# Layer 2 of the last sample as side steps of layer 3, with layer 3's preparation on one PSUM bank

## The chip, the core and the metric

The kernel runs on one core of one Trainium2 chip. The metric is the device time of one execution in microseconds (us). The kernel before took 10504.44 us, the median of three runs (10501.73, 10504.44 and 10507.75).

The engines are named as in the profile: PE is TensorE (matmul), DVE is VectorE, ACT is ScalarE, POOL is GpSimd, SP is SyncE, which here issues all DMAs. Each engine works through its own queue in order, and waits at an instruction until what it needs is there.

## What is computed

Four layers on images x of shape (4 samples, 128 channels, 64 x 64 pixels), in float32. Cut to what matters here:

```
# layer 2, for each sample, n = 4096 pixels
f, g, hh = Wf x + bf, Wg x + bg, Wh x + bh        # 1, 1 and 128 rows of n
attn = softmax(f[i] * g[j], over j)               # n x n, rank one before the softmax
out  = hh @ attn + x                              # bcj,bji->bci

# layer 3: two Mamba scans over all 4 x 4096 pixels as one sequence, forward and backward
u, z  = split(Win x);  u = silu(conv(u, 4 taps) + conv_b)
dt, B, C = Wx u;  delta = softplus(Wdt dt + bdt)
h[l] = exp(delta[l] A) * h[l-1] + delta[l] B[l] u[l]    # 256 channels x 16 states
y = (C . h + D u) * silu(z);  y = Wout y
out = silu(groupnorm(y_forward + y_backward)) + x       # groups of one sample
```

The forward scan of layer 3 reads the samples in order 0, 1, 2, 3. It needs the last sample's layer 2 only in its last quarter.

## The kernel before

**The scan stream** (scan_stream, L715) is used by layers 1 and 3. The work is cut into blocks of 128 rows by 1024 pixels (8 channels x 16 states). For block i, in this order: ACT copies the last column of h of block i-2 to `carry` (carried, L811); PE spreads the inputs of block i+1 to a PSUM pair of banks, `db` (spread, L749; two such pairs); ACT makes `da` of block i+2, an exponential (decayed, L758; three buffers), or, of each fourth block ("apart"), turns `db` itself into the decay (decayed_apart, L762); SP loads the row of block i+3 (load_for, L774; five buffers); DVE multiplies `db` with `b_rep` and runs the scan into `h` (four buffers); POOL multiplies row with `b_rep` to `x` for the apart blocks (driven, L783) and h with `c_rep` to `p` (seven buffers); PE sums p of four blocks into `total` with the matrix `gather` (summed, L795). After each block the caller's `side` runs, and before each scan its `early`. In these both, steps of other work are put into the engines' queues at places that are written out by hand or taken from a queue of steps. The order on each engine is the order of the program.

**Layer 1** has 256 blocks per sample. Beside them run the next window's preparation, the finished window's output (finish, L1149), and layer 2 of the sample before: pass_a (L1432), run eight times in finish, makes g, h, f and the extremes of g for 512 pixels each; row_weights (L1471), beside layer 0 of the next sample, makes the sums of the softmax; attend (L1511), beside layer 1 of the next sample, makes the 256 exponentials of 128 x 512 and their 256 matmuls, 16 results `res` on DVE, and stores to x3. The last sample has no next one, so finish leaves pass_a out for it, and layer2 (L1593) runs between layer 1 and layer 3 by itself: it loads the whole sample, makes g and h, and then, for 32 groups of 128 pixels, one exponential of 128 x 4096 on ACT with its sum, and eight f32 matmuls of 512 columns into eight PSUM banks, and at the end eight additions and eight stores to x3.

**Layer 3** (L1671) loads its weights (weights3, L1642: 47 small and middle-sized DMAs on SP, 32 of them for A_log), prepares chunk 0, and streams 32 chunks of 1024 pixels, 16 forward and 16 backward, each as two parts j of 16 blocks. A chunk is prepared (prep, L1717) beside the chunk before it; a table gives the block in which each step is issued. For each j: four taps of the convolution in two halves of 512 pixels and a Silu from PSUM (u); the rows of B, C and dt (bc); the time step with Softplus from PSUM (de, delta); the gate z with Silu from PSUM; then time_steps (L863), in steps: `du = delta u` on POOL, the stores of `d`, a copy of 32 rows, the first cast to bfloat16 (`high`), two rounds of remainders on PE and ACT (`minus`, `rest`), and `parted`, 12 DMAs of `split` to `parts`. Silu and Softplus need other ACT tables than the exponentials of the stream, so each of the six visits has two ACT_TABLE_LOADs, and uses two PSUM banks (ps1, two buffers). post (L1817) makes the output of the chunk before, and for the backward half finish reads y3 of a whole sample back, makes the group norm and stores the result; its buffers come from a pool `scratch` of two.

Of the kernel before, what the change touches and what calls it, by code (L numbers as in the profile page):

```python
# [16 lines left out]
P = 128  # L17
# [98 lines left out]
class Net:  # L116
# [186 lines left out]
    def weights12(self):  # L303
# [4 lines left out]
        self.load_rows(pool, ["bf", "bg", "bh"])  # L308
# [406 lines left out]
    def scan_stream(self, pools, blocks, side, early=lambda k, n: None):  # L715
# [95 lines left out]
        def carried(i):  # L811
            B, g = of(i)
            act.copy(B.carry[:, g : g + 1], h[i][:, B.at : B.at + 1])
            del h[i]
# [7 lines left out]
        for i, (k, n) in enumerate(items):  # L822
            B, g = of(i)
            if i > 1:
                carried(i - 2)
# [17 lines left out]
            pool.tensor_tensor(p[i], h[i], B.c_rep, ALU.mult)  # L843
            if n == 6 and k + 1 < len(blocks):
                blocks[k + 1].reps()
# [203 lines left out]
    def fetched(self, pool, b):  # L1049
        x = pool.tile([P, L], F32, name=f"x_{b}", tag="x")  # L1050
        for c in range(NCH):
            s = bass.ts(c, NB)
            self.nc.sync.dma_start(out=x[:, s], in_=self.x2[b % 2, :, s])
        return x


    def layer1(self, b):
# [12 lines left out]
        with self.pool("l1", 1) as big, self.pool("l1c", 2) as work, self.pool("l1t", 2) as tmp, \  # L1070
# [31 lines left out]
            def prepared(w):  # L1102
# [30 lines left out]
                for i in range(SG):  # L1133
# [3 lines left out]
                    g.way, g.at = slice(None), W - 1  # L1137
# [11 lines left out]
            def finish(w):  # L1149
# [26 lines left out]
                if not last:  # L1176
                    for c in range(C):
                        steps += self.pass_a(b, w * C + c, lambda c=c: held["x"][:, bass.ts(c, NB)], misc, tmp)
# [414 lines left out]
    def layer2(self, b, x):  # L1593
        nc = self.nc
        NT = L // P
        with self.pool("l2", 1) as big, self.pool("l2t", 2) as tmp, self.pool("l2e", 3) as ep:
            g = big.tile([P, L], F32, name="g", tag="g")
            hT = big.tile([P, NT, P], F32, name="hT", tag="hT")
            fcol = big.tile([P, NT], F32, name="fcol", tag="fcol")
            ntop = big.tile([P, NT], F32, name="ntop", tag="ntop")  # L1600
            gx = big.tile([P, 2, NCH], F32, name="gx", tag="gx")
            gm = big.tile([P, 2], F32, name="gm", tag="gm")
            with self.pool("l2p", 4, True) as ps4:
                for c in range(NCH):
                    s = bass.ts(c, NB)
                    ps = ps4.tile([P, NB], F32, name="g_ps", tag="misc")
                    nc.tensor.matmul(ps, self.wg_rep, x[:, s], start=True, stop=True)
                    nc.scalar.activation(g[:, s], ps, AF.Identity, bias=self.bg)
                    nc.vector.tensor_reduce(gx[:, 0, c : c + 1], g[:, s], AX.X, ALU.max)
                    nc.vector.tensor_reduce(gx[:, 1, c : c + 1], g[:, s], AX.X, ALU.min)  # L1610
                for t in range(NT):
                    ps = ps4.tile([P, NB], F32, name="h_ps", tag="misc")
                    nc.tensor.matmul(ps[:, 0 : P + 1], x[:, bass.ts(t, P)], self.WhfT, start=True, stop=True)
                    nc.vector.tensor_tensor(hT[:, t, :], ps[:, 0:P], self.bh, ALU.add)
                    nc.vector.tensor_tensor(fcol[:, t : t + 1], ps[:, P : P + 1], self.bf, ALU.add)
            nc.vector.tensor_reduce(gm[:, 0:1], gx[:, 0, :], AX.X, ALU.max)
            nc.vector.tensor_reduce(gm[:, 1:2], gx[:, 1, :], AX.X, ALU.min)

            nc.vector.tensor_scalar(ntop, fcol, gm[:, 0:1], None, ALU.mult)
            nc.vector.scalar_tensor_tensor(ntop, fcol, gm[:, 1:2], ntop, ALU.mult, ALU.max)  # L1620
            nc.vector.tensor_scalar(ntop, ntop, -1.0, None, ALU.mult)

            with self.pool("l2a", 1, True) as ps1:
                accs = [ps1.tile([P, NB], F32, name=f"acc{c}", tag=f"acc{c}") for c in range(NCH)]
                for t in range(NT):
                    e = ep.tile([P, L], F32, name="e", tag="e")
                    z = tmp.tile([P, 1], F32, name="z", tag="z")
                    nc.scalar.activation(
                        e, g, AF.Exp, bias=ntop[:, t : t + 1], scale=fcol[:, t : t + 1], accum_out=z,
                    )  # L1630
                    nc.vector.reciprocal(z, z)
                    nc.vector.tensor_scalar(hT[:, t, :], hT[:, t, :], z, None, ALU.mult)
                    for c in range(NCH):
                        nc.tensor.matmul(accs[c], hT[:, t, :], e[:, bass.ts(c, NB)], start=(t == 0), stop=(t == NT - 1))
                for c in range(NCH):
                    s = bass.ts(c, NB)
                    o = tmp.tile([P, NB], F32, name="o", tag="o")
                    nc.vector.tensor_tensor(o, accs[c], x[:, s], ALU.add)
                    nc.sync.dma_start(out=self.x3[:, b * L + c * NB : b * L + (c + 1) * NB], in_=o)


# [28 lines left out]

    def layer3(self):  # L1671
# [4 lines left out]
        with self.pool("l3w", 1) as big, self.pool("l3", 2) as work, self.pool("l3t", 2) as tmp, \  # L1676
                self.pool("l3x", 2) as scr, self.pool("l3u", 3) as st, self.pool("l3r", 2) as rows, \
                self.pool("l3p", 2, True) as ps1, self.pool("l3q", 2, True) as psd, \
                self.pool("l3s", 1, True) as pst:
# [14 lines left out]
            def scratch(name):  # L1694
                return scr.tile([P, T], F32, name=name, tag="s")
# [4 lines left out]
            def fetch(K):  # L1700

                lo = K.ch * T
                K.xt = work.tile([P, T + H], F32, name="xt", tag="xt")
                first, end = (lo - H, lo + T) if K.forward else (lo, lo + T + H)
                a, z = max(first, 0), min(end, N)
                if a > first:
                    dve.memset(K.xt[:, 0 : a - first], 0.0)
                if z < end:
                    dve.memset(K.xt[:, z - first : T + H], 0.0)
                sp.dma_start(out=K.xt[:, a - first : z - first], in_=self.x3[:, a:z])  # L1710

            def behind(K):

                K.yf = work.tile([P, T], F32, name="yf", tag="yf", bufs=1)
                sp.dma_start(out=K.yf, in_=self.y3[:, K.ch * T : (K.ch + 1) * T])

            def prep(K):  # L1717
# [3 lines left out]
                K.u = {}  # L1721

                def taps(j, c):
                    def go():
                        if c == 0:
                            K.u[j] = K.blocks[j].u = work.tile([P, T], F32, name="u", tag="u", bufs=3)
                        held["u", c] = misc("u_ps")
                        for i in range(self.K3):
                            o = c * NB + (i if K.forward else H - i)
                            pe.matmul(  # L1730
                                held["u", c], self.Wk[:, i, bass.ts(j, P)], K.xt[:, o : o + NB],
# [4 lines left out]
                def gate(j):  # L1736
                    def go():
                        if j == J - 1:
                            K.sz = work.tile([P, J, T], F32, name="sz", tag="sz")
                        for c in range(C):  # L1740
                            o = own + c * NB
                            held["z", c] = misc("z_ps")
# [345 lines left out]
```

## Time and profile before

| what | value |
|---|---|
| median of the three runs | 10504.44 us |
| profiled execution, span from its first to its last instruction | 10494.9 us |
| around the span, against the median of the runs | 9.5 us |
| mean granted TensorE clock | 0.903 |
| layer 1, first to last scan, samples 0, 1, 2, 3 | 861.3, 886.1, 883.6, 869.0 us |
| layer 3, first to last scan | 3463.9 us |
| DVE busy in layer 3 (6951 on): scans with `db`, products, scans apart | 1802.2, 926.8, 597.5 us |
| ACT_TABLE_LOADs of the whole kernel | 617 of 1283 ns |

How it is read: the profile's page gives, for one execution, the busy time of each engine, and the same in 40 slices of equal length (a digit 9 is 90% or more). Beside the page the trace can be asked for windows (busy time by engine in a stretch), for the timeline (start, duration, and in brackets the idle time before it and what ended it), for groups of equal instructions (count, busy time, mean duration, idle time before), and for waits. All times are in us from the first instruction. Nearly all rows carry the line L111, where a helper records every operation, so rows are told apart by their tiles. An f32 matmul leaves two records in the trace.

### The profile page before, as it was taken

Reading aid. Unit: us, or ns where it says so; the run is one execution under the profiler, and the core shown is the slowest. Engines: PE = TensorE matmul, PEld = TensorE weight load, DVE = VectorE, ACT = ScalarE, POOL = GpSimd, SP = SyncE. Lnnn points to the kernel's source line nnn. Section 1 sums busy time; section 2 is a strip of 40 time slices with the busy share of each in tenths; the row PEclk is TensorE's granted clock in tenths of the full one; section 3 lists DMA queues with packets and bytes.
Section 4 is the critical chain, followed back from the end, with each engine's and each line's share of the span. In section 5 each row is a group of like instructions: output and inputs, shape, how many; then the busy total and the mean of one; then the engine's idle time right before and its main releaser. Section 6 shows DMA issues by size and latency. Waiting matters only on the chain. (4 is left out here: it accounts for less than half of the span.)

```text
span 10494.9 us, 91078 instructions
## 1 busy us (share of the span) xinstructions
PE 8443.5 (80%) x28013; PEld 3021.6 (29%) x28088; DVE 9159.8 (87%) x6318; ACT 6387.1 (61%) x9576; POOL 8156.1 (78%) x3574
## 2 busy tenths in 40 slices
PE   8996667997887997887898887877777777777775
PEld 3331213332223333223333222322222222222221
DVE  7869998887998886999886999359999999999996
ACT  3334545666665665666665776456666666677765
POOL 6758896766887775888674888149999999989986
PEclk9997788998998999998999999888988989888886
DMA  1018882007885005887102888158888888888896
GB/s 37 12 37 201 194 194 85 18 14 189 211 203 149 15 14 129 201 213 191 33 16 63 206 211 200 32 133 199 207 198 206 204 202 208 215 223 224 228 227 176
DMA packets 512313, 1552.75 MB, mean 148 GB/s; under 512 B 84017, under 2 KB 91825, under 8 KB 511825
## 3 DMA queue, kind: packets, MB, share of 16 engines
q1 hardware_dynamic: 511824, 1546.92, 58.9%
q8 instruction: 223, 3.65, 0.2%
q14 instruction: 266, 2.17, 0.1%
HBM read 1349.40 MB, written 137.48 MB: 142 GB/s over the span
## 5 line engine op out<-in xcount | busy, mean ns | idle before, releaser
L111 POOL TENSOR_TENSOR p<-h,c_rep 128x1024 f32<-128x1024 f32 x2048 | 4807.9, 2359 | 734.8 <-DVE h L111 673.7
L111 DVE TENSOR_TENSOR_SCAN h<-da,carry,db 128x1024 f32<-128x1024 f32 x1536 | 3603.4, 2346 | 200.5 <-ACT da L111 17.8
L111 PE MATMUL db<-parts,sel 96*128 96x512 bf16 x4096 | 1401.5, 428 | 1460.3 <-DVE h L111 1408.2
L111 ACT ACTIVATE da<-row,A 128x1024 f32<-128x1024 f32 x1536 | 1761.1, 1147 | 359.4 <-DMA row<-d 341.0
L111 DVE TENSOR_TENSOR db<-b_rep,db 128x1024 f32<-128x1024 f32 x1536 | 1853.5, 1207 | 112.1 <-PE db L111 92.0
L111 POOL TENSOR_TENSOR e<-e,bound 128x1024 f32<-128x1024 f32 x512 | 1241.3, 2427 | 573.5 <-DVE e L111 573.0
L111 POOL TENSOR_TENSOR x<-row,b_rep 128x1024 f32<-128x1024 f32 x512 | 1208.8, 2361 | 123.8 <-DMA row<-d 122.8
L111 DVE TENSOR_TENSOR_SCAN h<-db,carry,x 128x1024 f32<-128x1024 f32 x512 | 1194.9, 2334 | 62.9 <-ACT db L111 35.3
L111 PE MATMUL total<-p,gather 128*32 128x512 f32 x8192 | 1225.7, 719 | 9.8 <-POOL p L111 9.8
L111 ACT ACTIVATE db<-db,A 128x1024 f32<-128x1024 f32 x512 | 555.3, 1085 | 1080.6 <-PE db L111 1026.5
L111 ACT ACTIVATE e<-e 128x1024 f32<-128x1024 f32 x512 | 540.9, 1057 | 1051.9 <-POOL e L111 1051.8
L111 PEld LDWEIGHTS <-sel 96*128 96x128 bf16 x4096 | 309.6, 101 | 3002.0 <-DVE h L111 2017.3
L111 PE MATMUL lg<-q,k 128*128 128x512 f32 x2048 | 1021.5, 623 | 106.5 <-DVE e L111 98.3
L111 PE MATMUL acc<-t,vT 128*128 128x512 f32 x2048 | 964.1, 595 | 3.3 <-DVE t L111 3.3
L111 PE MATMUL acc<-e,values 128*128 128x512 f32 x1536 | 854.9, 648 | 88.8 <-ACT e L111 62.9
L111 DVE TENSOR_TENSOR t<-lg,ncut 128x1024 f32<-128x1024 f32 x512 | 624.5, 1220 | 288.1 <-PE acc L111 264.0
L111 ACT ACT_TABLE_LOAD x617 | 791.6, 1283 | 38.8 <-DMA r<-y 12.3
L111 ACT ACTIVATE e<-gq,below,fcol 128x512 f32<-128x512 f32 x768 | 610.2, 805 | 87.0 <-PE acc L111 86.7
L111 POOL TENSOR_TENSOR t<-t,e 128x1024 f32<-128x1024 f32 x256 | 610.4, 2384 | 45.4 <-ACT t L111 45.4
L111 ACT ACTIVATE junk<-gp,ntop,fcol 128x512 f32<-128x512 f32 x768 | 619.5, 807 | 30.4 <-DMA gp<-g 17.7
L111 ACT COPY carry<-h 128x1 f32<-128x1 f32 x2048 | 373.5, 185 | 416.4 <-DVE h L111 411.4
L111 DVE SCALAR_TENSOR_TENSOR e<-t,lg 128x1024 f32<-128x1024 f32 x512 | 618.5, 1208 | 1.2
(259 smaller groups left out, 9927.5 us busy)
## 6 DMA issues: line engine op xcount, KB each, us to landing
row<-d SPq DMA_DIRECT2D x2048, 512.0 KB
parts<-split SPq DMA_DIRECT2D x912, 64.0 KB
b_rep<-bc SPq DMA_DIRECT2D x96, 512.0 KB
c_rep<-bc SPq DMA_DIRECT2D x96, 512.0 KB
d<-delta SPq DMA_DIRECT2D x76, 384.0 KB
r<-y SPq DMA_DIRECT2D x48, 512.0 KB
xq<-in_x SPq DMA_DIRECT2D x72, 256.0 KB
res<-x SPq DMA_DIRECT2D x32, 512.0 KB
```

Of the source, the lines that this page charges most:

```text
L111: return self.tc.keep_in_program_order(method(*args, **kwargs))
```

## The change

Five things are changed together.

1. layer2 and its loader are removed. finish of layer 1 runs pass_a for the last sample too. A new function, layer2_beside, does the rest as side steps of layer 3's forward blocks: 128 exponentials of 128 x 1024 with their sums (store), a logarithm, then 256 exponentials of 128 x 512 and 256 f32 matmuls, two rounds of eight results, with loads from g2, h2, x2 and x3 and stores to x3. A list `busy` estimates ACT's time in each of the 32 blocks of a chunk, and a step is issued when the estimate leaves room in 3.3 us per block (up to 4.0 saved up). By the built order the 128 are issued in chunks 0 to 5 (22, then 26 in each of 1 to 4, then 2) and the 256 in chunks 5 to 11.
2. Its accumulator takes a PSUM bank of its own (psa), so layer 3's preparation has one bank instead of two. Each half of 512 is copied out by ACT at the beginning of a later block (`first`, a new hook of scan_stream), before the next half is made.
3. Of the six table visits per chunk, each two for u, delta and z become one: the halves are copied with their bias, and the function is then applied to whole tiles. So there are three visits, with six ACT_TABLE_LOADs instead of twelve.
4. In the forward half, the copy to `carry` is made by POOL, after p of block i, instead of ACT before it (512 copies of 128 x 1).
5. Buffers: xt 2 to 1, split of layer 3 2 to 1, `scratch` as two tags of one buffer each, yf used as the exponentials' buffer in the forward half; the steps of prep, post and finish are moved in their tables (`du` at blocks 16 and 18 instead of 15 and 21, the store of the chunk before at 11 instead of 8), and finish reads a sample's four parts in the opposite order.

```diff
-        self.load_rows(pool, ["bf", "bg", "bh"])
+        self.load_rows(pool, ["bf", "bh"])
+        self.load_rows(self.const, ["bg"])
...
         def carried(i):
             B, g = of(i)
-            act.copy(B.carry[:, g : g + 1], h[i][:, B.at : B.at + 1])
+            keep = pool.tensor_copy if B.carry_on_pool else act.copy
+            keep(B.carry[:, g : g + 1], h[i][:, B.at : B.at + 1])
             del h[i]
...
+            first(k, n)
-            if i > 1:
+            if i > 1 and not of(i - 2)[0].carry_on_pool:
                 carried(i - 2)
...
             pool.tensor_tensor(p[i], h[i], B.c_rep, ALU.mult)
+            if i > 1 and of(i - 2)[0].carry_on_pool:
+                carried(i - 2)
...
-                if not last:
-                    for c in range(C):
-                        steps += self.pass_a(...)
+                for c in range(C):
+                    steps += self.pass_a(...)
...
+    def layer2_beside(self, b, keep, e, g, psa, busy, per):
...
+        def steps():
+            load_row(0)
...
+            dve.tensor_scalar(ntop, fcol, gm[:, 0:1], None, ALU.mult)
+            dve.scalar_tensor_tensor(ntop, fcol, gm[:, 1:2], ntop, ALU.mult, ALU.max)
+            dve.tensor_scalar(ntop, ntop, -1.0, None, ALU.mult)
+            yield later(3)
+            for c in range(NW):
+                for t in range(NT):
+                    yield 1.42
+                    if t == HALF and c + 1 < NW:
+                        load_row(c + 1)
+                    act.activation(
+                        store[:, 1, :], row(c), AF.Exp, bias=ntop[:, t : t + 1], scale=fcol[:, t : t + 1],
+                        accum_out=sums[:, t, c : c + 1],
+                    )
...
+                for v in range(h * NCH, (h + 1) * NCH):
+                    for t in range(HALF):
+                        yield 0.81
+                        if t == HALF // 2:
+                            load_res(v)
+                            if v + 1 < 2 * NCH:
+                                load_part(v + 1)
+                        at = h * HALF + t
+                        act.activation(
+                            half(e, t), half(g, v), AF.Exp, bias=below[:, at : at + 1], scale=fcol[:, at : at + 1],
+                        )
+                        now["due"].append((v, t))
+
+        def product(v, t):
+            if t == 0:
+                acc[v] = psa.tile([P, NB], F32, name="acc", tag="acc")
+            pe.matmul(acc[v], values[:, t, :], half(e, t), start=(t == 0), stop=(t == HALF - 1))
...
+        def early(i):
+            v = now["full"]
+            if v is not None:
+                dve.tensor_tensor(res, acc.pop(v), res, ALU.add)
...
+            due, now["due"] = now["due"], []
+            for u in due:
+                product(*u)
+            now["left"] = min(now["left"] + per - busy[i % len(busy)], 4.0)
+            while now["need"] is not None and i >= now["from"] and now["need"] <= now["left"] and len(now["due"]) < 2:
+                now["left"] -= max(now["need"], 0)
+                now["need"] = next(run, None)
...
-                self.pool("l3x", 2) as scr, self.pool("l3u", 3) as st, self.pool("l3r", 2) as rows, \
-                self.pool("l3p", 2, True) as ps1, self.pool("l3q", 2, True) as psd, \
-                self.pool("l3s", 1, True) as pst:
+                self.pool("l3x", 1) as scr, self.pool("l3u", 3) as st, self.pool("l3r", 2) as rows, \
+                self.pool("l3v", 1) as keep, self.pool("l3p", 1, True) as ps1, self.pool("l3a", 1, True) as psa, \
+                self.pool("l3q", 2, True) as psd, self.pool("l3s", 1, True) as pst:
...
+                def whole(func, dst, last, bias):
+                    s = bass.ts(C - 1, NB)
+                    for j in (0, 1):
+                        if j != last:
+                            act.activation(dst(j), dst(j), func)
+                    rest = dst(last)[:, 0 : (C - 1) * NB]
+                    act.activation(rest, rest, func)
...
+                        act.activation(dst(last)[:, s], held["ps"], func, bias=bias[:, last : last + 1])
+                    self.exp_tables(act)
...
-                    0: [taps(0, 0)], 2: [taps(0, 1)], 3: [silu(0, "u")],
-                    7: [taps(1, 0)], 10: [taps(1, 1)], 11: [silu(1, "u")],
-                    12: [rows_a], 13: [rows_b], 14: [step_a(0), step_b(0)], 15: [rows_c, todo(0, 0)],
-                    16: [step_a(1), step_b(1)], 17: [todo(0, 1)],
-                    18: [gate(1), silu(1, "z")], 21: [todo(0, 2), todo(0, 3), todo(1, 0)],
-                    22: [todo(0, 4)], 23: [todo(0, 5), todo(1, 1)], 24: [todo(0, 6)],
-                    25: [todo(0, 7), todo(1, 2), todo(1, 3)], 26: [todo(0, 8), gate(0), silu(0, "z")],
-                    28: [todo(1, 4)], 29: [todo(1, 5)], 30: [todo(1, 6)], 31: [todo(1, 7)],
-                }, {1: [todo(1, 8)]}
+                first = {
+                    2: [u_half(0, 0)], 4: [u_half(0, 1)], 6: [u_half(1, 0)], 11: [rows_b(0)], 12: [rows_b(1)],
+                    13: [step_b(0, 0)], 14: [step_b(0, 1)], 15: [step_b(1, 0)],
+                    17: [z_half(1, 0)], 18: [z_half(1, 1)], 19: [z_half(0, 0)],
+                    22: [todo(0, 5)], 23: [todo(0, 7)], 24: [todo(0, 9)], 25: [todo(0, 11)],
+                    29: [todo(1, 5)], 30: [todo(1, 7)], 31: [todo(1, 9)], 32: [todo(1, 11)],
+                }
+                then = {
+                    0: [taps(0, 0)], 2: [taps(0, 1)], 4: [taps(1, 0)], 6: [taps(1, 1)], 7: [silu_u],
+                    10: [rows_a(0)], 11: [rows_a(1)], 12: [step_a(0, 0)], 13: [rows_c, step_a(0, 1)],
+                    14: [step_a(1, 0)], 15: [step_a(1, 1), softplus], 16: [gate(1, 0), todo(0, 0)],
+                    17: [gate(1, 1)], 18: [gate(0, 0), todo(0, 1), todo(1, 0)], 19: [gate(0, 1), silu_z],
+                    20: [todo(0, 2), todo(0, 3), todo(1, 1)],
+                    21: [todo(0, 4)], 22: [todo(0, 6)], 23: [todo(0, 8), todo(1, 2)], 24: [todo(0, 10)], 25: [todo(0, 12)],
+                    28: [todo(1, 3), todo(1, 4)], 29: [todo(1, 6)], 30: [todo(1, 8)], 31: [todo(1, 10)],
+                    32: [todo(1, 12)],
+                }
...
-                if i > 1:
-                    into(i - 2, {20: [lambda K=K: fetch(K)]})
+                if i:
+                    into(i - 2, {22: [lambda K=K: fetch(K)]})
...
-                slots = {4: [a(0)], 5: [b(0)], 6: [a(1)], 7: [b(1)], 8: [store]}
+                slots = {8: [a(0)], 9: [a(1)], 11: [store]}
```

`todo(j, i)` is step i of time_steps for part j: with the remainders halved, 0 is `du`, 1 the stores of d, 2 the copy of 32 rows, 3 the first cast, 4 to 11 minus and rest in turn, 12 `parted`.

## The prediction

> **What bounds the kernel now.** First the page's table of engines and its 40 slices, to see where no engine is full.
>
> ```profile
> PE 8443.5 (80%) x28013; PEld 3021.6 (29%) x28088; DVE 9159.8 (87%) x6318; ACT 6387.1 (61%) x9576; POOL 8156.1 (78%) x3574
> ...
> DVE  7869998887998886999886999359999999999996
> ACT  3334545666665665666665776456666666677765
> POOL 6758896766887775888674888149999999989986
> ```
>
> DVE is full (9) in 12 of the last 13 slices, layer 3, with POOL beside it. The one deep hole is slices 26 and 27 (DVE 3 and 5, POOL 1 and 4): layer 2 of the last sample and layer 3's start. The page's chain is cut into shares of 0%, so the path is read from the windows (us, us; then busy time and count of PE, PEld, DVE, ACT, POOL; clock, DMA share, GB/s) and the timeline.
>
> ```profile
> 6680.00:6860.00 180.00, 180.00 (x421) 79.72 (x420) 11.67 (x52) 100.12 (x52) 0.00 (x0) 1.00 0.00 0
> ...
> 7598.00:7860.00 262.00, 204.77 (x728) 67.11 (x731) 254.07 (x144) 170.91 (x249) 238.81 (x103) 0.92 0.84 203
> ```
>
> In layer 2 PE alone works (180 of 180 us), DVE 6%. In layer 3 DVE works 97%, POOL 91%, PE 78% at clock 0.92, ACT 65%.
>
> ```profile
> 6621.17 0.32 SPq L111 DMA_DIRECT2D x<-res  x1
> ...
> 6865.85 10.87 SPq L1639 DMA_DIRECT2D x<-o  x8
> ```
>
> ```profile
> 6951.65 1.23 DVE L111 TENSOR_TENSOR db<-b_rep,db 128x1024 f32<-128x1024 f32 x1 [54.55 <-PE db L111]
> ```
>
> The stretch that goes begins after the last store of layer 1 (6621.17) and ends with the issue of the last x3 store (6865.85 + 10.87 = 6876.72): **255.5 us**. From there to layer 3's first DVE work at 6951.65 are 74.9 us of weights and chunk 0's preparation, all before a full DVE.
>
> DVE sets layer 3's rate: three TENSOR_TENSOR and four scans take 13.05 us per four blocks (starts 1.34 and 2.26 us apart), so 104.4 per chunk of 32 blocks, and two `sz` of 1.2: 106.8. The timeline of DVE gives forward chunks of 106.4 to 108.9, mean 107.3. What keeps DVE waiting there adds to the time; what fills other engines does not.
>
> **The change, part by part.**
>
> *Layer 1's end.* pass_a now runs for the last sample too, eight times. Two runs stand after its last scan. Sample 2 has them: from `xc` at 4975.00 to the x2 store at 4986.69 are 11.7 us, sample 3 has 6617.16 to 6621.17, 4.0: **+7.7**. Six stand in the scan stream on a full DVE: two reductions 0.60 apart, and twice `values` with `fcol` at 0.54, is 2.3 each: **+13** (the two streams differ by 14.6 with the next sample's tokens in it; bounds 10 and 15).
>
> *Chunk 0's preparation* is serial, so the single PSUM bank costs here. Four u, two bc, four de and four z halves can't run ahead of the copy: 14 times a copy of 0.6 to 0.7 and two handoffs of 0.2, 15 us; six table loads less, 6 x 1.28 = 7.7 off; `split` with one buffer lets the second block's first cast start only when the 12 `parts` transfers of the first have landed, which take SP 9.5 us to issue now (6933.50 on) and of which I count 9. **+17** (bounds -8, only the loads, and +25, nothing saved). So DVE starts 255.5 - 7.7 - 13 - 17 = **218 us** earlier.
>
> *DVE in layer 3's forward half:* 16 `res<-acc,res` of 0.68 and eight small ones: **+13**.
>
> *Carry copies on POOL, 512 of them.* Two prices. Time on POOL: not in the trace; below, 0.034 (spacing of 128x1 memsets), above, 0.30 (128x128 affine select); I take 0.15, nearer the memset, as a copy reads too. The other is a new wait. Before, scan i waited for p(i-4) to give its h buffer back (four buffers). Now it waits for the carry copy of block i-4, which stands behind p(i-2) in POOL's queue, and p(i-2) needs scan i-2. POOL works 5 x 2.31 + 4 x 0.15 = 12.15 of 13.05 us, so it is on time by about 0.8. But both `du` (2.31 each) now stand at blocks 16 and 18, two blocks apart: POOL falls 4.6 behind, 0.8 is room and some 1.9 is idle time in which it catches up; the other 1.9 us DVE waits. 16 chunks: **+30** (with 0.034: 16; with 0.30: 50). Before, that lateness was covered by two more blocks.
>
> *The side steps.* By the built order chunks 0 to 4 hold 22 to 26 exponentials of 128x1024 each, chunks 5 to 11 the 256 of 128x512 (44 per full chunk) and as many f32 matmuls of two records; the last x3 store is in chunk 11, before chunk 12 is fetched. ACT's chunk was 76.5 us busy; off go 32 carries of 0.185 (5.9) and six loads (7.7), nine new copies of 0.58 to 0.69 add 5.9, longer merged passes save 0.5: 68. With 26 x 1.35 or 44 x 0.805 on top it is 103 of 107, and as ACT starts overlap by 0.08 us some 95 of real time. Of the 12 us left, 6.6 are waits for rows (105.4 us in 16 chunks): 12 `parts` issues hold up SP's queue for 11 to 13 us twice a chunk. SP gets up to 15 more DMAs a chunk, and DMA's share goes from 0.84 to about 0.90, what the backward half has now. PE: at full clock a chunk costs 53.8 us by records (0.429 f32, 0.215 bf16) and 14 for `total`, 68; 44 x 0.857 adds 38: **106 of 107** in chunks 6 to 10. A PE that is late delays `spread`, and that DVE. The nearest row with such steps is layer 1: 3.365 us per block without attend, 3.456 with it: 23.5 per 256 blocks, less 16 x 0.68 of DVE work, 12.7. Below: that, 15 with the large ones. Above: PE at the 0.92 of now, 106/0.92 = 115 per chunk, 7.6 x 6.2 = 47, and two row waits a chunk of 4.7 (ACT's timeline has one of 4.66) passed on to DVE in 11 chunks, 103: 150. I take 2 us in each of five and 4.5 in each of six chunks: **+37**, nearer the layer 1 row.
>
> *Costed at nothing in the stream.* With one bank, PE's taps, gates and rests wait for ACT's copy of the half before, and behind them in PE's queue stand `spread` and `summed`; the copies come first in a later block, so one to two blocks (3.3 us each) cover them. `split` with one buffer: the second cast stands three blocks, 10 us, behind `parts`, whose issue takes 11 to 13; ACT may wait 3 us with `da` behind it, which DVE sees only past ACT's lead of two blocks. `xt` with one buffer is loaded three blocks after its last reader. If ACT's lead is gone, these are part of the 150 above. Backward half: no carries, no side steps, ACT 2.3 us lighter: **0** (DVE waits 20.3 us for ACT's carries there, so -16; PE's waits for the bank at 2 us per chunk, +32). At the end, parts are read back oldest first, and the 12.3 us in which ACT waits for `r<-y` shrink: **-3**.
>
> Sum: -218 + 13 + 30 + 37 - 3 = **-141**. The profiled span 10494.9 becomes 10354; the runs' median 10504.4 stands 9.5 above that span, so the time is **10363**.
>
> **Rules weighed.** The row: two dependent DVE operations of one column, `shift` and `scale`, take 1.76 and 1.64 us beside POOL's work, `scale`'s reciprocal 0.14.
>
> ```profile
> L111 DVE SCALAR_TENSOR_TENSOR shift<-nmean,scale,gn_b 128x1 f32<-128x1 f32 x4 | 7.0, 1758 | 0.1
> ...
> L111 DVE RECIPROCAL scale<-scale 128x1 f32<-128x1 f32 x4 | 0.6, 144 | 1.4 <-ACT scale L111 1.4
> ```
>
> The Trainium skill, "GPSIMD Engine Reference", section 8 (Key points), says that GpSimd shares its SBUF interfaces with VectorE and contends with DVE instructions that have two SBUF inputs. That speaks against more work on POOL; but the scans here read one operand from PSUM, so by it the copies would be slowed little, and two small new DVE operations would cost 1.6 us each, 3 us in all. The row for a table load: 1.283 us, and the next activation starts 1.29 after it. "ScalarE: Activation LUTs", What ACT_TABLE_LOAD costs, adds a drain of 1.38 to each switch; by it the merge would free 16 us of ACT per chunk instead of 7.7, and the side steps would be cheaper than I say. No row here shows that drain.
>
> **Rivals.**
> 1. *All hides as in layer 1* (chance 0.2). For it: ACT's backlog is bounded by the plan. Forward cost 13 + 16 + 15 = 44, preparation +5: 10504 - 230 + 44 - 3 = 10315.
> 2. *PE or ACT becomes the bound in chunks 0 to 11* (0.22). For it: 106 of 107 us on PE, 95 on ACT with 6.6 of row waits. Against: PE held clock 1.00 when full. Forward cost 13 + 40 + 110: 10504 - 218 + 163 - 3 = 10446.
> 3. *Slower: the carry copy is dear on POOL* (0.06). POOL's chunk is 42 x 2.31 = 97 and 32 copies; past 0.75 us each the chunk exceeds 121, and 16 x 13.6 eats the 218. At 1.7, as DVE's small operations show, it is 151: 10504 - 218 + 16 x 44 = 10990. Against: memsets of one column take 0.10.
> 4. *The change doesn't do what it says* (0.02): the standing part goes, but an unseen wait at the join brings it back: about 10500.
>
> **The numbers.** My forecast has 0.5. From rivals 1 and 2 the range takes most: 10295 to 10455; it leaves out the unlikely ends of the unknown costs. A difference under 0.2% (21 us) this measurement can't tell from none. Faster 0.90, same 0.03, slower 0.07 (rival 3 and the far end of 2).
>
> **What would show it.** No window with PE alone between layers; the first DVE work of layer 3 near 6734; forward chunks of about 111 (0 to 4), 114 (5 to 11) and 109 (12 to 15), backward as now near 109; scans whose wait ends with POOL's carry, after blocks 16 to 22; POOL copies near 0.15. Wrong would be: a chunk over 121, copies over 0.3, a preparation past 120 us, or a backward half that changes by over 30.

## The result and the profile after

The changed kernel takes **10624.82 us** (median of four runs, 10623.23 to 10640.98), against 10503.08 us for the kernel before in the same session: a ratio of 1.0119, 95% interval 1.0105 to 1.0133. It is 1.2% slower, where 1.3% faster was forecast. The profiled execution has a span of 10639.2 us, 144.3 more than the one of before; it is the slowest of its four, so the differences below add up to 144.3 where the medians differ by 121.7. One execution further below, the profiled one of experiment 1, took 10768.31 us at a granted clock of 0.786 where the other three had 0.885 to 0.887, and is left out there. By stages, from the starts and ends of scans in the two traces:

| stage (us) | before | after | difference | forecast |
|---|---|---|---|---|
| up to layer 1's last scan | 6611.3 | 6634.6 | +23.4 | +13 |
| from there to layer 3's first scan | 342.0 | 121.8 | -220.2 | -231 |
| chunks 0 to 4 | 538.9 | 570.4 | +31.5 | all forward +80 |
| chunks 5 to 11 | 748.5 | 962.4 | **+213.8** | |
| chunks 12 to 15 | 428.8 | 446.4 | +17.6 | |
| chunks 16 to 31 (backward) | 1747.6 | 1821.3 | **+73.7** | 0 |
| after the last scan | 77.7 | 82.4 | +4.7 | -3 |

The part that stood alone is gone, and nearly as much as forecast was gained there. The scans of layer 3 give it all back and 116 more. The page's slices of the changed kernel (one digit is a fortieth of the span, 266 us) show where:

```profile
PE 8594.6 (81%) x28088; PEld 2985.4 (28%) x28088; DVE 9163.4 (86%) x6233; ACT 6461.4 (61%) x9513; POOL 8219.9 (77%) x4086
...
DVE  7869998878998987998886999598777999999996
ACT  3334545656665665665665665687666556666664
POOL 6758886757887775887775888598767998888886
```

The deep hole of two slices has shrunk to one digit 5. Behind it DVE stands at 7 for three slices (7447 to 8245 us): these are chunks 6 to 11, with the exponentials and products of the second phase. In the last third POOL is at 8 where it was at 9: the backward half, which has no side steps at all, is slower too.

First the chunks of the products. The windows of the changed kernel, for chunks 6 to 10 (us; busy time and count of PE, PEld, DVE, ACT, POOL; clock, DMA share, GB/s), and what its DVE and its ACT waited for there (total us, times, longest):

```profile
7453.30:8169.00 715.70, 613.22 (x1897) 210.32 (x1896) 533.83 (x304) 489.63 (x579) 510.37 (x371) 0.93 0.65 168
```

```profile
DVE h L111 <- ACT db L111: 68.6, 29, 7.1
DVE db L111 <- PE db L111: 54.9, 40, 3.2
DVE res L111 <- PE acc L111: 36.9, 11, 5.2
...
DVE h L111 <- POOL carry L111: 1.4, 2, 0.9
```

```profile
ACT yf L111 <- PE acc L111: 163.3, 95, 4.7
```

A chunk takes 143.1 us instead of 107.1. No engine fills it: per chunk PE is busy for 122.6 us, DVE for 106.8, ACT for 97.9. DVE waits for ACT's decay of the apart blocks (`h <- ACT db`), for PE's spread and for the accumulator. ACT waits 163.3 us for PE before its exponentials: each writes a half of `yf`, and waits until the product that read this half is done. The timeline of PE and then of ACT in one stretch of the changed kernel (start, duration, in brackets the idle time before and what ended it) shows that the two take turns:

```profile
7509.41 1.98 PE L111 MATMUL acc<-yf,store 128*128 128x512 f32 x4
7511.23 0.60 PE L111 MATMUL db<-parts,sel 96*128 96x512 bf16 x2
7512.83 1.91 PE L111 MATMUL bc_ps<-u,Wbcd 128*40 128x512 f32 x4 [1.00 <-ACT bc L111]
7514.67 1.98 PE L111 MATMUL acc<-yf,store 128*128 128x512 f32 x4
```

```profile
7510.62 1.68 ACT L111 ACTIVATE yf<-gq,below,fcol 128x512 f32<-128x512 f32 x2 [1.86 <-PE acc L111]
7512.21 0.56 ACT L111 COPY bc<-bc_ps 40x512 f32<-40x512 f32 x1
7512.68 1.15 ACT L111 ACTIVATE da<-row,A 128x1024 f32<-128x1024 f32 x1
7515.89 1.67 ACT L111 ACTIVATE yf<-gq,below,fcol 128x512 f32<-128x512 f32 x2 [2.07 <-PE acc L111]
```

Read it as a ring. As the two products end (7510.6 and 7511.4), the two exponentials may write `yf` (7510.62 to 7512.30); then ACT copies `bc` out of the only bank (to 7512.77); then PE may make the next `bc_ps` (7512.83 to 7514.74), behind which the next two products stand (to 7516.65), and with the first of these come the next exponentials (7515.89). One turn is 5.3 us. PE's own work in it is 4.5, ACT's 3.4, and DVE needs 3.3 per block.

In the backward half the waits before DVE's scans of chunks 17 to 30 are, before (two lines) and after (one):

```profile
DVE h L111 <- ACT carry L111: 20.3, 15, 4.1
DVE h L111 <- ACT db L111: 6.1, 6, 2.1
```

```profile
DVE h L111 <- ACT db L111: 80.0, 34, 7.9
```

Put down by the block in which they fall, these waits stand in front of scans 23 and 31 of a chunk (2.4 and 2.8 us in the mean of chunks 16 to 30, under 0.3 and 1.0 before), in chunks 0 to 4 and 12 to 15 also of scan 22 (1.3 us, behind POOL's carry copy; 0.1 before). Blocks 23 and 31 are apart blocks.

### The profile page after: what moved, and what is told of

Same layout as the page of the kernel before. It is cut to its first block, busy times and chain, and to the rows that moved or that the text cites. A ratio compares the mean times of both kernels' runs of the same rounds, so it can differ in the third digit from the quotient of the medians.

```text
span 10639.2 us, 91843 instructions
## 1 busy us (share of the span) xinstructions
PE 8594.6 (81%) x28088; PEld 2985.4 (28%) x28088; DVE 9163.4 (86%) x6233; ACT 6461.4 (61%) x9513; POOL 8219.9 (77%) x4086
## 5 line engine op out<-in xcount | busy, mean ns | idle before, releaser
L111 PE MATMUL lg<-q,k 128*128 128x512 f32 x2048 | 1019.6, 622 | 106.9 <-DVE e L111 100.9
L111 DVE TENSOR_TENSOR t<-t,fl 128x1024 f32<-128x1024 f32 x512 | 615.8, 1209 | 3.9 <-PE fl L111 3.9
```

What stands on the lines that cost most here:

```text
L111: return self.tc.keep_in_program_order(method(*args, **kwargs))
```

## The experiments

All kernels are changes of the changed kernel. A difference is taken between medians; the ratios are to the kernel before in the same session. Where the preparation has two banks (5, 7 to 11), `scale` of finish also stands one block earlier (53 instead of 54).

**1. No side steps.**

```diff
-                if chunks[k // J].forward:
-                    beside(i)
+                if 64 <= i < 68: sp.dma_start(out=<x3, last sample, part i - 64>, in_=<the same of x2>)
...
-                if chunks[k // J].forward:
-                    early(k * NS + n)
+                pass
```

> The changed kernel without its side steps: no exponentials, products and stores of layer 2 for the last sample beside layer 3 (its x3 is filled with x2 by four copies from DRAM to DRAM in blocks 64 to 67 of the stream, so this part of the output is another). Theory A, the side steps cost the time of chunks 0 to 11: all forward chunks take 111.6 us as chunks 12 to 15 do now (0 to 4 now 114.1, 5 to 11 now 962.3 in sum), total 12 + 181 us lower, about 10430. Rival, something else than the side steps (clock, DMA) slows chunks 0 to 11: they stay over 114, total over 10470. In both, chunks 12 to 31 stay at 111.6 and 113.9, which would show that the preparation itself costs 4.5 us per chunk over the kernel before.

Measured: 10439.35 us, the median of three; ratio 0.9939 (0.9922 to 0.9955). The side steps cost 185 us, as theory A has it (the sum expected 193). But without them the kernel gains only 69 us on the one before, out of about 200 at the join: what else was changed in layer 3, in all 32 chunks, costs the rest, 130 to 145 by these times and by the traces (4.4 us per chunk in chunks 12 to 15, 4.6 in the backward half).

**2. Carry copies back on ACT.**

```diff
-    B.rows, B.carry_on_pool = self.d3[K.turn, j], forward
+    B.rows, B.carry_on_pool = self.d3[K.turn, j], False
```

> The changed kernel with the copies to carry back on ACT in the forward half. Theory A, the POOL copy's only price is the wait of scan 22 behind the two du: 1.3 us less in each of the forward chunks that ACT does not bind, 0 to 4 and 12 to 15, so 12 us less there; in chunks 5 to 11, where ACT and PE wait for each other, 32 copies of 0.19 more on ACT make them 2 to 6 us longer each: total 0 to +30. Rival, the POOL copies are what makes the forward half slow: forward chunks fall by 4 us or more each, total 64 or more lower, and chunks 5 to 11 with them.

Measured: 10628.74 us, 4 above the changed kernel. Chunks 1 to 4 take 112.6 (113.8 with POOL's copies). The copies are no cause: they take 0.185 us on POOL and 0.183 on ACT. With them on ACT scan 22 no longer waits (1.2 to 0.1 us in chunks 0 to 4, 1.3 to 0.1 in 12 to 15), but scan 23 behind it waits longer (1.8 to 3.5, and 0.6 to 2.1).

**3. The preparation's copies behind the decays of the block.**

```diff
-            first(k, n)
             if i > 1 and not of(i - 2)[0].carry_on_pool:
...
             decayed_apart(i + 1)
+            first(k, n)
             load_for(i + AHEAD)
```

> The changed kernel with the hook of the preparation's copies moved in ACT's queue from the beginning of the block to behind the two decays of the block. Theory A, the copies stand ahead of the decay of the apart block, which has no lead, and each waits for its matmul: the waits of scans 23 and 31 go, chunks 16 to 31 fall from 113.9 to about 110, 12 to 15 from 111.6 to about 109.5, chunks 5 to 11 by as much or more: total 90 to 130 lower. Rival, the merged visits make ACT late (five us at blocks 7, 15 and 19), and the copies only show it: chunks 12 to 31 change by under 1 us each, total within 20.

Measured: 10886.28 us, 261 *above* the changed kernel; both theories fall. Chunks 6 to 10 go from 143 to 167, backward chunks from 114 to 118. ACT's decays wait for PE's spread, so copies put behind them come later, and with one bank PE's next matmul waits for the copy. PE's waits of chunks 17 to 19, in the changed kernel and in this one:

```profile
PE db L111 <- DVE h L111: 47.3, 45, 3.0
PE rest_ps L111 <- ACT split L111: 5.6, 9, 3.1
```

```profile
PE db L111 <- DVE h L111: 20.7, 19, 3.0
PE rest_ps L111 <- ACT split L111: 12.4, 13, 1.7
PE u_ps L111 <- ACT u L111: 10.7, 6, 1.8
```

PE waits less for DVE, which is harmless, and more for ACT's copies (`u` is new in the list), with `spread` queued behind. With one bank neither of the two orders serves both: the bank has to be emptied early for PE, and the decay comes late by it.

**4. The products ahead of the preparation's matmuls.** The loop over `due` moves from the end of the block (`beside`) to before its scan (`early`):

```diff
         def early(i):
...
+            due, now["due"] = now["due"], []
+            for u in due:
+                product(*u)
```

> The changed kernel with the side steps' products put into PE's queue ahead of the preparation's matmuls of the block (after the spread) instead of behind them. Theory A, chunks 5 to 11 are a ring: an exponential waits for the product that frees its half of the buffer, the product stands behind a matmul of the preparation, which waits for ACT's copy, which stands behind the exponentials of the block before; with the products ahead the ring is cut, chunks 6 to 10 fall from 143 to 120 to 128, total 90 to 150 lower. Rival, PE's throughput is the bound (122 us of records per chunk at the clock of 0.93 and the load of weights between them): the order does not matter, chunks 6 to 10 stay at 140 to 146, total within 20.

Measured: 10541.87 us (ratio 1.0031, 1.0018 to 1.0043), **83 below** the changed kernel; chunks 6 to 10 take 126.5. Only the order in PE's queue was changed, so the ring is shown. The same two views, for chunks 6 to 10 of this kernel:

```profile
ACT yf L111 <- PE acc L111: 64.2, 38, 3.9
```

```profile
7441.50:8073.80 632.30, 582.47 (x1897) 208.86 (x1896) 532.52 (x305) 485.99 (x579) 510.77 (x371) 0.95 0.75 191
```

ACT's wait before the exponentials is 99 us shorter, and PE is now busy 582.5 of 632.3 us, 92%. What is left, 126.5 against the 111.6 of chunks without side steps, is near PE's load, as the rival has it; that this load is all of it is not shown.

**5. The idle bank given to the preparation, without side steps.**

```diff
-    self.pool("l3p", 1, True) as ps1, self.pool("l3a", 1, True) as psa
+    self.pool("l3p", 2, True) as ps1
```

> The kernel without side steps (the first experiment; the last sample's part of layer 2 is left out in the same way), with the PSUM bank that is then idle given to the preparation: two buffers instead of one, all else equal. Theory A, the single bank is what makes each chunk 4.5 us longer than before: forward chunks fall from 112.4 to 108.5, backward ones from 113.9 to 110, and chunk 0's preparation from 102 to about 90 us: total 110 to 140 below that experiment, 10300 to 10335. Rival, the merged visits and the halved remainders do it: chunks stay over 111.5, total over 10405.

Measured: 10391.54 us, 48 below experiment 1 (110 to 140 were expected, so theory A is too strong). The stretch from layer 1's last scan to layer 3's first goes from 121.8 to 100.9 us, 21 of the 48. In the chunks the bank is worth about 1 us each: 1.6 in the backward half (1796.0, after the change 1821.3), less in the forward one. Scans 23 and 31 still wait 2.3 and 2.1 us in the backward half. ACT's timeline before scan 31 of a chunk in this kernel tells why:

```profile
8936.31 1.14 ACT L111 ACTIVATE da<-row,A 128x1024 f32<-128x1024 f32 x1
8943.10 1.04 ACT L111 CAST split<-du 128x1024 bf16<-128x1024 f32 x1 [5.65 <-DMA parts<-split]
8944.82 0.59 ACT L111 CAST split<-rest_ps 128x512 bf16<-128x512 f32 x1 [0.67 <-PE rest_ps L111]
...
8947.80 0.59 ACT L111 CAST split<-rest_ps 128x512 bf16<-128x512 f32 x1 [2.31 <-PE rest_ps L111]
...
8951.49 1.09 ACT L111 ACTIVATE db<-db,A 128x1024 f32<-128x1024 f32 x1 [1.97 <-PE db L111]
```

The cast of the second part waits 5.65 us for the transfers that read the one buffer of `split`; the decay of block 31 comes at 8951.49, and its scan starts 5.65 us after the one before it, where 2.3 is usual for an apart block. Before scan 23, PE's first remainder waits for ACT's copy of 32 rows (8915.59 to 8916.63), which stands behind the merged visit of block 19 (its second table load ends at 8914.31), and PE's spread of block 23 is queued behind the remainder:

```profile
8916.68 2.08 PE L111 MATMUL rest_ps<-du,ident 128*128 128x512 f32 x2 [1.72 <-ACT du L111]
8918.55 0.63 PE L111 MATMUL rest_ps<-split,minus 128*128 128x512 bf16 x1
8919.11 2.16 PE L111 MATMUL total<-p,gather 128*32 128x512 f32 x16
8921.21 0.60 PE L111 MATMUL db<-parts,sel 96*128 96x512 bf16 x2
```

**6, 7, 8. With the whole computation: one exponential per block, and the second bank while no products run.** All three have the products ahead.

```diff
-    ... and now["need"] <= now["left"] and len(now["due"]) < 2:
+    ... and (now["need"] <= now["left"] or now["need"] == 0.81) and len(now["due"]) < 1:
```

```diff
             def misc(name, rows=P):
+                bank[0] = 1 - bank[0] if quiet[0]() else 0
+                if bank[0]:
+                    return psa.tile([rows, NB], F32, name=name, tag="acc")
                 return ps1.tile([rows, NB], F32, name=name, tag="misc")
```

> The changed kernel with the products ahead of the preparation's matmuls, and at most one exponential per block in the second phase (so it lasts 7.4 chunks instead of 6). Theory A, what is left of the ring is the second exponential of a block, which waits for a product of the same block: chunks 6 to 12 take 114 to 117 instead of 126.5, total about 50 below the kernel with the products ahead alone, 10480 to 10500. Rival, the load itself on ACT and PE costs 0.32 us per exponential: chunks of 122.5, two more of them, total 10530 to 10550.

> As the one before (products ahead, one exponential per block), and the preparation uses the bank of the side steps as a second one while no products run: chunks 0 to 4 and 13 on. Theory A (one bank costs 3.5 to 4 us per chunk, in 24 chunks, and some 12 in chunk 0's preparation): 90 to 105 below the one before: 10380 to 10405, faster than the kernel before. Rival (merged visits cost it): within 25 of the one before.

> Products ahead, up to two exponentials per block as in the change, and the second bank while no products run: chunks 0 to 4 and 11 on. Theory A: 95 to 110 below the kernel with the products ahead alone, 10430 to 10450; chunks 6 to 10 stay at 126.5. Rival: within 25 of it.

Measured: one exponential 10536.92 (5 below experiment 4, chunks of 122.8, two more of them: the rival's numbers); one exponential and banks 10496.14 (ratio 0.9991, 0.9981 to 1.0000); two exponentials and banks 10493.34 (0.9989, 0.9980 to 0.9998). An exponential with its product costs 0.34 or 0.35 us of time, 44 or 32 to a chunk. The second bank brings 41 and 49, half of what was expected, in line with experiment 5: 18 to 21 in chunk 0's preparation, the rest in the chunks.

**9. The three handoffs, without side steps.** `split` as three tiles of a plane each; the first part's remainders one block later, and in blocks 22, 26 and 30 behind the decays; the second `du` at block 21:

```diff
-    lambda: tmp.tile([P, 3, T], BF16, name="split", tag="split", bufs=1),
+    lambda: Planes([tmp.tile([P, T], BF16, name=f"split{i}", tag=f"split{i}", bufs=1) for i in range(3)]),
...
-    22: [todo(0, 5)], 23: [todo(0, 7)], 24: [todo(0, 9)], 25: [todo(0, 11)],
+    23: [todo(0, 5)], 24: [todo(0, 7)], 25: [todo(0, 9)], 26: [todo(0, 11)],
...
-    18: [gate(0, 0), todo(0, 1), todo(1, 0)],
+    18: [gate(0, 0), todo(0, 1)], 21: [todo(1, 0)],
```

> The kernel without side steps and with two banks (layer 2 of the last sample left out as there), and three edits for the three blocks in which its scans still wait: split as three tiles of one plane each, so that the cast of the second part waits only for the four transfers of the first plane (scan 31: 1.7 us forward, 2.1 backward); the remainders of the first part one block later, and in blocks 22, 26 and 30 behind the decays (scan 23: 0.2 and 2.3); du of the second part at block 21 instead of 18 (scan 22: 1.3 in forward chunks). Theory A, these three handoffs are the rest of the loss per chunk: forward chunks fall from 111.2 to about 108, backward ones from 112.3 to about 109 (107.3 and 109.2 before), total 10270 to 10310. Rival, the merged visits (5 us of ACT at a time) move the waits to other scans: chunks fall by under 1 us, total over 10360.

Measured: 10308.32 us (ratio 0.9812, 0.9799 to 0.9826), 83 below experiment 5: theory A. Forward chunks take 108.8, backward ones 110.0 in the mean; in chunks 6 to 9 the wait before scan 22 is at its floor of 0.13 (1.3 in experiment 5) and those before 23 and 31 are at 0.0 and 0.1 (0.7 and 0.9), in chunks 17 to 29 at 1.1 and 0.6 (2.3 and 2.0). DVE's waits in chunks 17 to 30, in experiment 5 and here:

```profile
DVE h L111 <- ACT db L111: 57.0, 28, 3.3
```

```profile
DVE h L120 <- ACT db L120: 34.3, 21, 2.6
```

80.0 us in the changed kernel, 57.0 with two banks, 34.3 here. The three edits were not tried one by one on two banks, so the 83 us belong to them together. The merged visits stay, so of the loss they can hold at most what is left over the kernel before, 1.5 us per forward and 0.8 per backward chunk; that they make ACT late enough for the other handoffs to show is plausible and wasn't tried by itself.

**10, 11. The whole computation with all of it.** Experiment 8 with the edits of 9; and the same with a table for the exponentials:

```diff
+            some = 2 if n > 23 else n not in (7, 8, 15, 18, 19, 20, 21, 22)
```

> The whole computation: products ahead, the second bank while no products run, and the three edits of the kernel above. Theory A: 60 to 100 below the kernel with the first two, 10395 to 10435, and faster than the kernel before. Rival: over 10460.

> As the one before, with the exponentials of the second phase given by a table: none in blocks 7, 8, 15 and 18 to 22, where a table visit holds ACT, two in blocks 24 to 31, one in the others. Theory A, exponentials beside the visits cost more than 0.32 us each: chunks of the second phase fall from 126 to under 120, 20 to 60 below the one above. Rival, each costs the same wherever it stands: within 15 of it.

Measured: 10423.01 us (ratio 0.9921, 0.9908 to 0.9935) and **10413.65 us** (0.9907, 0.9893 to 0.9920). Both beat both kernels, the second by 93 us the one before it all. The table makes chunks of 119.7 instead of 123.5, under the 120 of theory A, but with 32 exponentials in place of 44, so about two more such chunks are needed, and the total is the rival's: the 9 us between the two are within their intervals. Over the chunks without side steps an exponential still costs 0.34 us in the first and 0.36 in the second. The page's slices of the second:

```profile
DVE  7869998887998886999887899699888899999996
...
POOL 6758886766887775888675788599888899988986
```

**12. Only the planes of `split`, on the changed kernel.**

```diff
-    lambda: tmp.tile([P, 3, T], BF16, name="split", tag="split", bufs=1),
+    lambda: Planes([tmp.tile([P, T], BF16, name=f"split{i}", tag=f"split{i}", bufs=1) for i in range(3)]),
```

> The changed kernel with one edit: the single buffer split becomes three tiles of one plane each (the same memory), so that the cast of a chunk's second part waits for the four transfers of the first plane and not for all twelve. Theory A, the single buffer is the cause of the wait before scan 31 (1.9 us in chunks 0 to 4, 2.1 in 6 to 10, 2.8 in the backward half): it falls below 1, 30 to 55 lower in all, 10570 to 10595, and chunk 0's preparation is some 4 us shorter. Rival, the single PSUM bank makes scan 31 late by itself: the wait stays over 1.3, total within 20.

Measured: 10614.38 us, 10 below the changed kernel, not the 30 to 55 of theory A. In chunks 0 to 4 the wait before scan 31 goes from 1.9 to 0.1 us, and in each of chunks 11 to 20 it is 0.0; in chunks 6 to 10 it stays at 2.1. The cast's wait in chunk 17, where scan 31 waits 2.2 us in the changed kernel and 0.0 in this one:

```profile
8946.12 1.04 ACT L111 CAST split<-du 128x1024 bf16<-128x1024 f32 x1 [5.70 <-DMA parts<-split]
```

```profile
8917.44 1.04 ACT L120 CAST split<-du 128x1024 bf16<-128x1024 f32 x1 [0.46 <-DMA parts<-split]
```

So theory A has the cause of this wait right, but not its worth. In the backward half the mean goes only from 2.8 to 2.0: 24 of the 30 us left stand in chunks 22, 26 and 30, where a normalisation of finish comes between the casts (in chunk 22 ACT waits 5.18 us for `r<-y` before the table load for it, at 9487.62). And part of the gain moves to other scans: over all chunks the waits before scan 31 fall by 31 us, those before scans 15 and 23 grow by 12 (scan 23 from 1.8 to 2.6 in chunks 0 to 4). The second bank without the planes brings 48 us (experiment 5), the planes without the bank 10, and experiment 9, with both and a later order of the steps, 83 more than the bank. That each handoff is in part hidden by the others fits all three, but no run has just the bank and the planes.

## Why the prediction was wrong, step by step

Two terms of the sum failed: the side steps, and the handoffs of the preparation, which were put at nothing. Of the prediction's four signs of being wrong two came, chunks over 121 us (143) and a backward half that changes by over 30 (73.7); the copies (0.185) and the preparation (102.4) stayed inside theirs.

- **The standing part, -255.5:** right. It is gone (PE alone was full there, but ACT was also busy for 100 of the 180 us shown), and layer 1's tail grew by 7.8 (7.7 forecast).
- **Six pass_a in the stream, +13:** right. Layer 1 of the last sample, first to last scan, went from 869.0 to 885.6, +16.6, but it has the same steps in the profiles of the changed kernel and of experiments 2 to 12, and there it takes 877.0 to 885.6, 881.6 in the mean: +12.6. The other 6.8 us of the first row of the table come before that sample's layer 1, where nothing was changed; they are the difference of two executions.
- **Chunk 0's preparation, +17 (bounds -8 and 25):** from the first weight to DVE's first work are 102.4 us, +27.4. With two banks (experiment 5) they are 81.4, so the single bank costs 21, where copies and handoffs were counted as 15, and all else costs 6.5, where 2 were counted. Left out of the 15 is PE's clock, which was lower with the single bank (below).
- **Carry copies, +30:** 0.185 us each (0.15 taken), and the wait that was named, behind both `du`, is there: 1.3 us before scan 22 (1.9 taken), but only in nine of the 16 chunks. Some 10 us by these waits, and none by experiment 2, where scan 23 waits instead. Rival 3 had its condition at 0.75 us.
- **The side steps, +37, and 13 for DVE's work in them:** this is the step that failed worst: 185 for the 50. ACT's load was right (103.0 per chunk as a sum of durations and 97.9 of real time; 103 and 95 counted), PE's a little low (106 at full clock, 116.5 of records at 0.95). The failure was to take the price from layer 1's stream, 23.5 us for 256 exponentials. Here each writes a buffer of two halves, with products queued behind matmuls that wait for ACT: each engine's load was set against the chunk's 107 us by itself, where a ring between two engines sets the time. The ring is 83 of the 185 (experiment 4). Some 102 stay without it, still twice the forecast: 0.34 us per exponential instead of 0.09, and as much with one in a block as with two (experiment 6). Rival 2 had chunks 5 to 11, and its 10446 for the total is still 179 short; it named the throughput of PE or ACT, and that can only be what is left once the ring is cut.
- **"Costed at nothing in the stream" and "Backward half: 0":** the second failure, some 140 us in all 32 chunks (4.4 to 4.6 each). The prediction saw each handoff: the copies before PE's next half, the cast that waits for `parts`, by 3 us. It covered them with ACT's lead of two blocks. That lead is of `da`. The decay of an apart block has none: it needs the spread of its own block, which needs the `db` pair that the scan two blocks before gives back. In an undisturbed block of experiment 5 the decay starts at 8933.27, ends at 8934.36, and the scan starts at 8936.09: 1.7 us of room, where one cast alone was 5.65 us late. The bound of "+32" for the bank in the backward half held: of the 73.7 us there, 25 went with the second bank (experiment 5) and 35.5 with the three edits of experiment 9, whose handoffs the prediction had put at nothing; 13 are left, and their cause is open.
- **The tail, -3:** +4.7. ACT's idle time before its table loads there, of which the 12.3 us of waits for `r<-y` were to shrink, grew from 18.4 us to 23.4, three waits for `r<-y` of 7.7 to 7.8.
- **The merged visits:** ACT's 68 us per chunk came out as 67.9 (chunks 12 to 15). The fewer loads freed ACT's time, of which there was enough.
- **The two rules weighed:** the two small DVE operations on few columns at the start of the stream took 1.47 and 2.28 us beside POOL, 3.8 together, near the 3 of the row; they end at 6760.39 and 6762.71, as POOL's `x` and `p` do (6760.37 and 6762.68), and the two like them right behind take 0.25 and 0.18. The tables still show 1.28 us per load with the activation 1.29 after its start, as in the trace of before; no profile here shows a drain of 1.38.

Not tried: the six separate visits with one bank, the edits of experiment 9 one by one, or more halves for the exponentials. How much of the remaining 11 to 15 us per chunk in the second phase is PE's load alone is therefore open; PE is busy 93% of it in experiment 10 (572.96 of 617.3 us).

## What to carry to other kernels

When work of a second kind is put beside a full stream, draw its ring: which buffer an instruction waits for, what stands ahead of the one that frees it in the other engine's queue, and what that waits for. Loads that fit in the time of each engine say nothing while two engines take turns on one bank and two halves; an order that puts the freeing instruction ahead of unrelated work cost nothing and brought 83 us. And "the lead of two blocks covers it" has to be said per instruction: the one with the shortest lead sets the room for everything that stands ahead of it in its queue.

## What the runs showed of the hardware

PE's clock in the serial preparation of chunk 0. In the changed kernel the windows of its first and second part are:

```profile
6674.00:6703.00 29.00, 22.36 (x42) 7.76 (x42) 0.00 (x0) 8.46 (x11) 0.00 (x0) 0.88 0.05 15
6703.00:6755.00 52.00, 33.46 (x45) 8.93 (x46) 0.00 (x0) 23.02 (x30) 4.64 (x2) 0.57 0.39 98
```

The granted clock falls from 0.88 to 0.57 as PE waits 0.67 us or more for each copy, and the same matmul goes from 1.12 to 2.07 us within 2 us of time:

```profile
6703.33 1.12 PE L111 MATMUL de_ps<-bc,Wdt 8*128 8x512 f32 x2 [0.78 <-ACT delta L111]
6705.23 2.07 PE L111 MATMUL de_ps<-bc,Wdt 8*128 8x512 f32 x2 [0.78 <-ACT delta L111]
```

Before, with two banks, the like stretch (6900 to 6951) was granted 0.91 and 0.69, and with two banks in experiment 5 (6667 to 6726.8) 0.85 and 0.70. The Trainium skill, "TensorE: Matmul & The Clock Gate", Part 1 and "HAM oscillation — how this bites in real kernels", says that the array runs at half rate when it has not been busy lately, and that waits between bursts bring it back there. The trace agrees: 1.12 to 2.07 is near a factor of two. The waits that brought it down here were short: none of PE's from 6676 to 6705 is longer than 0.86 us. So a single bank costs twice at such a place, by the handoffs and by the slower matmuls; how the 21 us divide between the two is not shown.
